# The first attention's softmax: query maxima by GpSimd's partition_all_reduce, row sums by more products with ones

## The chip, the core and the metric

The program runs on one core of a Trainium2 chip. The metric is the device time of one execution in microseconds (us). The time before is 1392.51 us, the median of 3 runs (1391.57 to 1392.85). Five engines work side by side, each with its own queue of instructions: TensorE (PE, with its weight loads as PEld), VectorE (DVE), ScalarE (ACT), GpSimd (POOL) and SyncE (SP, which issues DMAs). A name with a q, such as POOLq, is the engine's sequencer.

## The reference

The whole network is four layers of attention, mixing and feed-forward blocks over x of 4 x 128 x 128. The change touches only the first block, an attention with ternary weights over 2048 context rows for each of the 4 batches. `bitnet_linear` is a product of rounded inputs with ternary weights.

```python
vis = bitnet_linear(dinov2_features, W_d2v, b_d2v)
image_embeds = bitnet_linear(vis, W_img, b_img)
fused = bitnet_linear(text_embeddings, W_txt, b_txt)
for Wa, ba in ((W_att0, b_att0), (W_att1, b_att1)):
    kv = bitnet_linear(image_embeds, Wa, ba)
    k = jnp.concatenate([kv, kv], axis=-1)
    scores = jnp.einsum('bse,bpe->bsp', fused, k) * inv_sqrt_e
    attn = jax.nn.softmax(scores, axis=-1)
    fused = fused + 0.1 * jnp.einsum('bsp,bpe->bse', attn, k)
```

So for two rounds and four batches there is a softmax of 128 queries over 2048 keys, and its product with the keys themselves. The second round starts from the first round's result.

## The kernel before, in words

The block is `bit_attention` (from L935). It quantizes the context, makes the keys of both rounds (`k_ps` L1053 evicted by ACT at L1056, `v_ps` L1061 evicted by DVE at L1063), and then works through 8 units, one for each round and batch (L1148 on). A unit has its 2048 keys on the partitions, as 16 chunks of 128 keys; the 128 queries lie along the free dimension. Eight chunks make one PSUM tile `st` of 128 x 1024, so a unit has two halves, g = 0 and 1. For one unit:

- `queries` (L1078 to L1082): a product with `fold`, DVE scales it into `fq`; then DVE adds 0.1 times the key bias to `fused`.
- `scores` (L1092, L1094): 8 products into `st` for a half, and a DVE reduction over the 8 chunks into `mh`: for each partition and query the largest score.
- `top` (L1097 to L1101): DVE joins the two halves of `mh` (L1097); PE transposes it so that the queries lie on the partitions (`m_tr` L1099), and DVE takes the maximum for each query (`mq` L1101).
- `spread` (L1104, L1106): PE transposes `mq`, repeated 128 times, back (L1104), and ACT copies the result to SBUF as `mb`: the maximum of each query on every partition.
- `weights` (L1110 to L1120), for each half: DVE subtracts `mb` from `st` into `p` (L1110), ACT takes exp (L1112), and GpSimd adds up the eight chunks of `p` in three additions of 128 x 512, 128 x 256 and 128 x 128 (L1118, L1119, L1120) into `total`. For the last unit DVE does these additions.
- `values` (L1135 to L1145), one unit behind: 16 products `av` of `p` with the keys, two products of `total` with ones (`rsum` L1140), DVE's reciprocal and product (L1142, L1143), a product with `fold` (L1144), and DVE adds the result into `fused` (L1145).

The pipeline over the units is written out at the bottom: `top` of unit i, first half of the scores of unit i + 1, `spread` and `weights` of unit i, `values` of unit i - 1, second half of the scores of unit i + 1, `queries` of unit i + 2. After unit 2 comes `ternary(ps, 5, 7)`, which makes the ternary weights for the feed-forward (ACT sums at L960, product L965, DVE L966 to L974). After units 3 and 4 GpSimd turns a stretch of the mask into floats (`ctxT`, L1175). `st` has three PSUM buffers, the small tiles have two. After the units the largest magnitude of `fused` is found by DVE (L896, L900) and GpSimd (L903), and the feed-forward follows (L1198 on).

The order of the instructions on an engine is near the order of the source, but not the same: the framework that builds the program places an instruction earlier where its buffers allow. It also puts a pair of `MODIFY_POOL_CONFIG` records on GpSimd's queue wherever a `PARTITION_ALL_REDUCE` follows an addition or scaling by GpSimd, or the other way round. In the source nothing of this is seen; in the instruction order of a program it stands as one extra entry on GpSimd ahead of the first instruction of the new kind. Memsets and copies have none.

Of the kernel before, what the change touches and what calls it, by code (L numbers as in the profile page):

```python
# [9 lines left out]
F32 = mybir.dt.float32  # L10
BF16 = mybir.dt.bfloat16
# [3 lines left out]
ALU = mybir.AluOpType  # L15
AX = mybir.AxisListType.X
PSUM = bass.MemoryType.PSUM

P = 128
B = 4  # L20
T = 128
# [250 lines left out]
class Net:  # L272
# [662 lines left out]
    def bit_attention(self, nxt):  # L935


        nc, tc = self.nc, self.tc
        w = self.load("l0x")
        with ExitStack() as es:  # L940
            one = es.enter_context(tc.tile_pool(name="bit1", bufs=1))
            wk = es.enter_context(tc.tile_pool(name="bit2", bufs=2))
# [39 lines left out]
            ps = es.enter_context(tc.tile_pool(name="bit_ps", bufs=2, space=PSUM))  # L982
# [29 lines left out]
            total = one.tile([P, NS // W], F32, name="total")  # L1012
# [24 lines left out]
            HC = NCH // 2  # L1037
            rounds = []
            for r, n in enumerate(("att0", "att1")):
                kv = big.tile([P, BIG], F32, tag="big", name="kv")  # L1040
                kT = kv[:, 0 : NS // 2]
                v = kv[:, NS // 2 :].rearrange("p (c w) -> p c w", w=64)
                osc = out_scale(n, s_img)
                osc10 = self.small(1, "osc10" + n)
                nc.vector.tensor_scalar_mul(osc10, osc, 0.1)
                rounds.append((n, kT, v, osc10))
                pairs = qimg.rearrange("p (c h k) -> p c h k", h=2, k=P)
                for j in range(B):
                    mm = stp.tile([P, W], F32, tag="st", name="k_ps")
                    for lo in range(0, W, 512):  # L1050
                        at = (j * W + lo) // P
                        for h in range(2):
                            nc.tensor.matmul(  # L1053
                                mm[h * 64 : h * 64 + 64, lo : lo + 512], qw[:, L0X[n]], pairs[:, at : at + 4, h],
                                start=True, stop=True)
                    nc.scalar.activation(  # L1056
                        kT[:, j * W : j * W + W], mm, AF.Identity, bias=self.col("b_" + n), scale=osc)
                    mm = stp.tile([P, W], F32, tag="st", name="v_ps")
                    for i in range(NCH):
                        at = (j * NCH + i) * P  # L1060
                        nc.tensor.matmul(  # L1061
                            mm[:, i * 64 : i * 64 + 64], qimg[:, at : at + P], qw[:, L0X[n]], start=True, stop=True)
                    nc.vector.tensor_copy(  # L1063
                        v[:, j * NCH : j * NCH + NCH], mm.rearrange("p (c w) -> p c w", w=64))

            class Unit:
# [2 lines left out]

                def __init__(u, r, b):  # L1070
                    u.b = b
                    u.n, u.kT, u.v, u.osc10 = rounds[r]
                    u.fb = fused[:, b * T : b * T + T]
                    u.st, u.ts = [None, None], []

                def queries(u):
                    mm = ps.tile([P, 512], F32, tag="mm", name="fq_ps")
                    nc.tensor.matmul(mm[:, 0:T], self.flat(fold), u.fb, start=True, stop=True)  # L1078
                    u.q = wk.tile([P, T], F32, tag="fq", name="fq")
                    nc.vector.tensor_scalar_mul(u.q, mm[:, 0:T], 1.0 / math.sqrt(C))  # L1080
                    nc.vector.scalar_tensor_tensor(
                        u.fb, self.col("b_" + u.n).to_broadcast([P, T]), 0.1, u.fb, ALU.mult, ALU.add)  # L1082
                    u.mh = wk.tile([P, 2, P], F32, tag="mh", name="mh")
                    u.total = wk.tile([P, 2, P], F32, tag="total", name="total")

                def scores(u, g):
                    u.st[g] = stp.tile([P, 2, HC // 2, P], F32, tag="st", name="st")
# [7 lines left out]

                def top(u):
                    nc.vector.tensor_max(u.mh[:, 0], u.mh[:, 0], u.mh[:, 1])  # L1097
                    u.mm = ps.tile([P, 512], F32, tag="mm", name="m_tr")
                    nc.tensor.transpose(u.mm[:, 0:P], u.mh[:, 0], self.ident)  # L1099
                    u.mq = self.small(1, "mq")  # L1100
                    nc.vector.reduce_max(u.mq, u.mm[:, 0:P], axis=AX)  # L1101

                def spread(u):
                    nc.tensor.transpose(u.mm[:, P : 2 * P], u.mq.to_broadcast([P, P]), self.ident)  # L1104
                    u.mb = wk.tile([P, P], F32, tag="mb", name="mb")
                    nc.scalar.copy(u.mb, u.mm[:, P : 2 * P])  # L1106

                def weights(u, g):
                    p = tp.tile([P, HC, P], F32, tag="p", name="p")
                    nc.vector.tensor_sub(  # L1110
                        p, u.st[g].rearrange("p h c q -> p (h c) q"), bc_mid(u.mb, HC))
                    nc.scalar.activation(p, p, AF.Exp)  # L1112
                    u.ts.append(p)

                    half = p[:, 0 : HC // 2]
                    a = wk.tile([P, HC // 2, P], F32, tag="qtmp", name="psum")
                    eng = nc.vector if u is units[-1] else nc.gpsimd
                    eng.tensor_add(a, half, p[:, HC // 2 :])  # L1118
                    eng.tensor_add(a[:, 0:2], a[:, 0:2], a[:, 2:4])  # L1119
                    eng.tensor_add(u.total[:, g], a[:, 0], a[:, 1])  # L1120

                def values(u):
                    def bank(name):

                        if u is units[-1]:
                            return stp.tile([P, W], F32, tag="st", name=name)
                        return ps.tile([P, 512], F32, tag="mm", name=name)


                    av = bank("av")  # L1130
                    for g in range(2):
                        for c in range(HC // 2):
                            for h in range(2):
                                ch = u.b * NCH + 2 * (g * (HC // 2) + c) + h
                                nc.tensor.matmul(  # L1135
                                    av[h * 64 : h * 64 + 64, 0:T], u.v[:, ch], u.ts[g][:, h * (HC // 2) + c],
                                    start=g + c == 0, stop=g == 1 and c == HC // 2 - 1)
                    mm = bank("rsum")
                    for g in range(2):
                        nc.tensor.matmul(mm[:, 0:T], self.ones, u.total[:, g], start=g == 0, stop=g == 1)  # L1140
                    o = wk.tile([P, T], F32, tag="o", name="o")
                    nc.vector.reciprocal(o, mm[:, 0:T])  # L1142
                    nc.vector.tensor_mul(o, o, av[:, 0:T])  # L1143
                    nc.tensor.matmul(mm[:, T : 2 * T], self.flat(fold), o, start=True, stop=True)  # L1144
                    nc.vector.scalar_tensor_tensor(u.fb, mm[:, T : 2 * T], u.osc10, u.fb, ALU.mult, ALU.add)  # L1145

            units = [Unit(r, b) for r in range(2) for b in range(B)]
# [4 lines left out]
            for i, u in enumerate(units):  # L1152
                u.top()
                if i + 1 < len(units):
                    units[i + 1].scores(0)
                u.spread()
                u.weights(0)
                u.weights(1)
                if i:
                    units[i - 1].values()  # L1160
                if i + 1 < len(units):
                    units[i + 1].scores(1)
                if i + 2 < len(units):
                    units[i + 2].queries()
                if i == 2:
                    ternary(ps, 5, 7)
                if i in (3, 4):

                    half = NS // 2
                    lo = (i - 3) * half  # L1170
                    mw = wk.tile([P, 1024], I32, tag="qtmp", name="mask")
                    nc.sync.dma_start(
                        mw[DC:AUG], self.A["mask"][:, lo // 4 : (lo + half) // 4].partition_broadcast(3)[:, 0])
                    aug = self.k("augs")[DC:AUG]
                    nc.gpsimd.tensor_scalar(  # L1175
                        self.ctxT[DC:AUG, lo : lo + half], mw.bitcast(U8)[DC:AUG], aug[:, 0:1], aug[:, 1:2],
                        ALU.mult, ALU.add)
# [10 lines left out]
            self.quantize(wk, fused, qf, inv)  # L1188
            qa = one.tile([P, B], BF16, name="qa")
            self.quantize(wk, avg, qa, inv)  # L1190
            qab = one.tile([P, B, T], BF16, name="qab")
            nc.vector.tensor_copy(qab, bc_in(qa, T))
            hT = big.tile([P, BIG], F32, tag="big", name="hT")[:, 0 : 4 * N].rearrange("p (m n) -> p m n", m=4)
            osc = out_scale("f1", s)
# [1056 lines left out]
```

## Time and profile before

| What | Value |
|---|---|
| Median of 3 runs | 1392.51 us |
| Profiled execution's own time | 1393.84 us |
| Its span, first to last instruction | 1391.7 us |
| Mean granted TensorE clock over the span | 0.916 |
| The units' stretch, 85.9 to 151.4 us: DVE busy | 50.90 of 65.50 us |
| The same: PE busy | 48.82 us |
| The same: POOL busy | 41.39 us |
| The same: ACT busy | 19.86 us |
| The same: granted TensorE clock | 0.81 |

In a line of the timeline the columns are start, busy time, engine, line, operation, output and inputs, and in square brackets how long the engine had been idle and what ended that. In a table of groups, a count, the busy time and the mean ns of one stand ahead of the idle time. In a table of waits each row is the waiting engine and tile, what it waited for, the total in us, the number of times and the longest.

The eight copies of `mb` (L1106) start at 85.68, 93.64, 102.65, 114.82, 125.59, 135.08, 143.16 and 151.11 us. They mark the beat of the units.

### The profile page before, as it was taken

The page shows a single profiled execution, that of the slowest core. Times are in us where ns is not written, and L with a number is a line of the kernel's source. Part 1 is how long each engine was busy: PE and PEld are TensorE (multiplying, and loading weights), DVE is VectorE, ACT ScalarE, POOL GpSimd, SP SyncE. Part 2 cuts the span into 40 slices and gives each one's busy share as a digit, 9 for nine tenths or more (in the row PEclk, how much of TensorE's full clock was granted, in tenths as well). Part 3 has the DMA queues.
Part 4 walks back from the last instruction along what each step waited for, and adds up shares of the span by engine and source line. Part 5 has one row for each costly group of instructions (what it writes and reads, how often), then busy time and mean ns, then how long its engine had stood idle before and what let it go on. Part 6 is the DMA issues. An engine that isn't in the chain of part 4 may idle for free.

```text
span 1391.7 us, 15803 instructions
## 1 busy us (share of the span) xinstructions
PE 1149.7 (83%) x6204; PEld 604.2 (43%) x6204; DVE 914.2 (66%) x1596; ACT 627.0 (45%) x848; POOL 205.9 (15%) x187
## 2 busy tenths in 40 slices
PE   2477557677899999999998944899987889999978
PEld 0156422222644444444433424476342454666644
DVE  7988779899348666776676698512564776554535
ACT  3743256444346555665553410233542761545432
POOL 0026205357000001000000430000122200000000
PEclk9988768789999999999999976799998988999978
DMA  6000000000700000000000100330000000000010
GB/s 188 0 1 2 1 1 0 30 0 0 211 0 1 0 0 0 1 0 0 1 1 0 61 0 1 104 75 23 0 0 7 7 7 0 2 1 2 3 57 8
DMA packets 9485, 27.82 MB, mean 20 GB/s; under 512 B 1191, under 2 KB 7120, under 8 KB 8350
## 3 DMA queue, kind: packets, MB, share of 16 engines
q1 hardware_dynamic: 8286, 24.88, 6.2%
q10 hardware_dynamic: 1120, 1.88, 0.4%
q8 instruction: 51, 0.84, 0.3%
q14 instruction: 28, 0.23, 0.1%
HBM read 26.49 MB, written 0.26 MB: 19 GB/s over the span
## 4 chain that ended last, share of the span: by engine, by line
PE 61%; DVE 19%; ACT 5%; issue 5%; POOL 3%; DVEq 0%; ACTq 0%; POOLq 0%
PE sc L590 12%; PE av L614 12%; PE s_ps L780 5%; DVE h L1392 3%; PE t_ps L804 2%; PE k_ps L706 2%; PE h_ps L1831 2%; PE y_ps L1843 2%; PE av L817 2%; PE mm L1478 2%; PE y_ps L1397 1%; DVE dbu L1383 1%; PE q_ps L542 1%; POOL hc L1395 1%; POOL mbs L606 1%
## 5 line engine op out<-in xcount | busy, mean ns | idle before, releaser
L614 PE MATMUL av<-s,ctx 128*97 128x512 f32 x448 | 210.4, 601 | 11.6 <-ACT s L612 11.0
L590 PE MATMUL sc<-q_aug,ctxT 99*128 99x512 f32 x448 | 206.2, 592 | 0.0
L611 DVE TENSOR_TENSOR s<-s,mbs 128x1024 f32<-128x1024 f32 x112 | 133.0, 1220 | 39.0 <-POOL mbs L606 39.0
L592 ACT COPY s<-sc 128x1024 f32<-128x1024 f32 x112 | 112.3, 1003 | 80.7 <-PE sc L590 80.7
L612 ACT ACTIVATE s<-s 128x1024 f32<-128x1024 f32 x112 | 116.2, 1057 | 63.1 <-DVE s L611 62.8
L600 DVE TENSOR_TENSOR m<-m,s 128x1024 f32<-128x1024 f32 x72 | 88.2, 1225 | 75.0 <-ACT s L592 75.0
L590 PEld LDWEIGHTS sc<-q_aug,ctxT 99*128 99x128 f32 x448 | 84.6, 189 | 110.2 <-issue 91.3
L614 PEld LDWEIGHTS av<-s,ctx 128*97 128x97 f32 x448 | 72.5, 166 | 124.1 <-issue 103.6
L784 DVE TENSOR_REDUCE na_m<-s_ps 128x1 f32<-128x512 f32 x128 | 82.2, 686 | 61.9 <-PE s_ps L780 61.7
L606 POOL PARTITION_ALL_REDUCE mbs<-m x20 | 35.7, 1785 | 488.4 <-DVE m L602 488.4
L810 ACT ACTIVATE p<-t_ps 128x1024 f32<-128x1024 f32 x64 | 62.0, 1021 | 85.4 <-PE t_ps L804 85.4
L1397 PE MATMUL y_ps<-hc,consts 128*128 128x512 f32 x128 | 75.6, 724 | 29.2 <-POOL hc L1395 27.7
L1395 POOL TENSOR_TENSOR hc<-h,cs 128x1024 f32<-128x1024 f32 x32 | 75.7, 2378 | 84.1 <-DVE h L1392 84.1
L780 PE MATMUL s_ps<-kT,q 32*128 32x512 f32 x256 | 81.9, 682 | 1.0 <-DVE na_m L784 0.9
L1392 DVE TENSOR_TENSOR_SCAN h<-dA,dbu 128x512 f32<-128x512 f32 x64 | 74.2, 1205 | 4.1 <-ACT dA L1389 3.9
L1397 PEld LDWEIGHTS y_ps<-hc,consts 128*128 128x128 f32 x128 | 26.1, 223 | 82.0 <-POOL hc L1395 56.4
L804 PE MATMUL t_ps<-q,kT 32*128 32x128 f32 x1024 | 57.0, 287 | 1.2 <-ACT p L810 1.2
L1389 ACT ACTIVATE dA<-delta,A 128x508 f32<-128x508 f32 x64 | 42.8, 687 | 29.5 <-DVE h L1392 29.3
L804 PEld LDWEIGHTS t_ps<-q,kT 32*128 32x128 f32 x1024 | 48.6, 189 | 11.2 <-issue 7.0
L393 PEld LDWEIGHTS <-consts 128*128 128x128 bf16 x160 | 17.6, 120 | 67.4 <-issue 51.3
L1847 DVE SCALAR_TENSOR_TENSOR x<-y_ps,cw,x 128x128 f32<-128x128 f32 x32 | 9.0, 345 | 50.3 <-PE y_ps L1843 44.4
L780 PEld LDWEIGHTS s_ps<-kT,q 32*128 32x128 f32 x256 | 28.1, 194 | 25.4 <-DVE na_m L784 14.8
(599 smaller groups left out, 1949.5 us busy)
## 6 DMA issues: line engine op xcount, KB each, us to landing
w_moe<-in_moe SPq DMA_DIRECT2D x2, 2048.0 KB, 9.6
ctxT<-in_ctxT SPq DMA_DIRECT2D x3, 768.0 KB
w_l3f<-in_l3f SPq DMA_DIRECT2D x1, 1920.0 KB, 8.1
rows<-in_rows ACTq DMA_DIRECT2D x1, 1664.0 KB, 13.7
w_l0f<-in_l0f SPq DMA_DIRECT2D x1, 1024.0 KB
w_mamba<-in_mamba SPq DMA_DIRECT2D x1, 976.0 KB, 18.3
w_r<-in_r SPq DMA_DIRECT2D x1, 960.0 KB
consts<-in_consts SPq DMA_DIRECT2D x1, 832.0 KB, 16.6
```

The lines of the kernel that those rows point to most:

```text
L590: nc.tensor.matmul(sc[:, i], self.ctxT[:, at : at + P], u.q, start=True, stop=True)
L592: nc.scalar.copy(s, sc)
L600: nc.vector.tensor_max(u.m, u.m, u.s[j])
L611: nc.vector.tensor_sub(p, p, bc_mid(u.mb, 2))
L612: nc.scalar.activation(p, p, AF.Exp)
L614: nc.tensor.matmul(u.av[: DC + 1], self.ctx[:, u.b * NCH + chunks[2 * j + i]], p[:, i], start=j + i == 0, stop=j == n - 1 and i == 1)
L780: nc.tensor.matmul(t, qs[rows], kT[rows, s, j * 512 : j * 512 + 512], start=True, stop=True)
L784: nc.vector.tensor_reduce(part[:, at : at + 1], t, axis=AX, op=ALU.max, negate=True)
L804: nc.tensor.matmul(ts[g // 2][:, g % 2, j], kT[g * 32 : g * 32 + 32, s, at : at + P], qs[g * 32 : g * 32 + 32], start=True, stop=True)
L1392: nc.vector.tensor_tensor_scan(h[:, half], self.flat(dA), dbu[:, half], 0.0, ALU.mult, ALU.add)
L1395: nc.gpsimd.tensor_mul(hc, h, bc_mid(cs, 2))
L1397: nc.tensor.matmul(y[:, half], self.ident, hc[:, half], start=n == 0, stop=n == 15)
```

## The change

`top` now ends with one GpSimd `partition_all_reduce` of 128 x 128, which takes the maximum over the partitions and writes it to all of them as `mb`; the two transposes, `mq` and the copy by ACT are gone, and `spread` with them. Of the three additions by GpSimd for each half only the first is left; `total` is four times as large, and `values` sums its eight chunks with eight products with ones in place of two. For the last unit there are no additions at all, and 16 products with ones. Two smaller edits: the key bias times 0.1 is made once for a round (`b01`), so that the addition to `fused` is a `tensor_scalar`; and `qab` shares a buffer.

```diff
+                b01 = self.small(1, "b01" + n)
+                nc.vector.tensor_scalar_mul(b01, self.col("b_" + n), 0.1)
...
-                    nc.vector.scalar_tensor_tensor(
-                        u.fb, self.col("b_" + u.n).to_broadcast([P, T]), 0.1, u.fb, ALU.mult, ALU.add)
+                    nc.vector.tensor_scalar(u.fb, u.fb, u.b01, None, ALU.add)
...
-                    u.total = wk.tile([P, 2, P], F32, tag="total", name="total")
+                    u.total = wk.tile([P, 2, HC // 2, P], F32, tag="total", name="total")
...
                     nc.vector.tensor_max(u.mh[:, 0], u.mh[:, 0], u.mh[:, 1])
-                    u.mm = ps.tile([P, 512], F32, tag="mm", name="m_tr")
-                    nc.tensor.transpose(u.mm[:, 0:P], u.mh[:, 0], self.ident)
-                    u.mq = self.small(1, "mq")
-                    nc.vector.reduce_max(u.mq, u.mm[:, 0:P], axis=AX)
-
-                def spread(u):
-                    nc.tensor.transpose(u.mm[:, P : 2 * P], u.mq.to_broadcast([P, P]), self.ident)
                     u.mb = wk.tile([P, P], F32, tag="mb", name="mb")
-                    nc.scalar.copy(u.mb, u.mm[:, P : 2 * P])
+                    nc.gpsimd.partition_all_reduce(u.mb, u.mh[:, 0], P, bass_isa.ReduceOp.max)
...
-                    half = p[:, 0 : HC // 2]
-                    a = wk.tile([P, HC // 2, P], F32, tag="qtmp", name="psum")
-                    eng = nc.vector if u is units[-1] else nc.gpsimd
-                    eng.tensor_add(a, half, p[:, HC // 2 :])
-                    eng.tensor_add(a[:, 0:2], a[:, 0:2], a[:, 2:4])
-                    eng.tensor_add(u.total[:, g], a[:, 0], a[:, 1])
+                    if u is not units[-1]:
+                        nc.gpsimd.tensor_add(u.total[:, g], p[:, 0 : HC // 2], p[:, HC // 2 :])
...
-                    for g in range(2):
-                        nc.tensor.matmul(mm[:, 0:T], self.ones, u.total[:, g], start=g == 0, stop=g == 1)
+                    if u is units[-1]:
+                        parts = [u.ts[g][:, c] for g in range(2) for c in range(HC)]
+                    else:
+                        parts = [u.total[:, g, c] for g in range(2) for c in range(HC // 2)]
+                    for c, v in enumerate(parts):
+                        nc.tensor.matmul(mm[:, 0:T], self.ones, v, start=c == 0, stop=c == len(parts) - 1)
...
-                u.spread()
...
-            qab = one.tile([P, B, T], BF16, name="qab")
+            qab = one.tile([P, B, T], BF16, tag="xn", name="qab")
```

In the instruction order of the new program GpSimd has, for the units: the all-reduce of unit 0, a pair of `MODIFY_POOL_CONFIG`, two additions of 128 x 512, a pair, the all-reduce of unit 1, a pair, two additions, and so on to the all-reduce of unit 7. The two conversions of the mask stand after the all-reduces of units 3 and 4, behind the pair and ahead of the additions. ACT's two sums for `ternary` (L960) stand ahead of the last five and the last three evictions of keys (L1056), where they stood between the exps of units 2 and 3.

More of the change, by code (lines that the diff above doesn't have):

```diff
@@ L1045, in bit_attention @@
                 nc.vector.tensor_scalar_mul(osc10, osc, 0.1)
-                rounds.append((n, kT, v, osc10))
+                b01 = self.small(1, "b01" + n)
+                nc.vector.tensor_scalar_mul(b01, self.col("b_" + n), 0.1)
+                rounds.append((n, kT, v, osc10, b01))
                 pairs = qimg.rearrange("p (c h k) -> p c h k", h=2, k=P)
@@ L1071, in __init__ @@
                     u.b = b
-                    u.n, u.kT, u.v, u.osc10 = rounds[r]
+                    u.n, u.kT, u.v, u.osc10, u.b01 = rounds[r]
                     u.fb = fused[:, b * T : b * T + T]
```

## The prediction

> **What bounds the kernel now.** The page's first part says who is busy over the whole span, and seems to invite the change: GpSimd has 15%.
>
> ```profile
> PE 1149.7 (83%) x6204; PEld 604.2 (43%) x6204; DVE 914.2 (66%) x1596; ACT 627.0 (45%) x848; POOL 205.9 (15%) x187
> ```
>
> The change acts in one stretch, so I read the timeline there, first for the steady units 6 and 7.
>
> ```profile
> 143.16 0.27 ACT L1106 COPY mb<-m_tr 128x128 f32<-128x128 f32 x1 [3.74 <-PE m_tr L1104]
> 144.06 2.35 DVE L1110 TENSOR_TENSOR p<-st,mb 128x1024 f32<-128x1024 f32 x2
> ...
> 146.32 0.95 DVE L1142 RECIPROCAL o<-rsum 128x128 f32<-128x128 f32 x1
> 146.44 1.26 POOL L1118 TENSOR_TENSOR psum<-p 128x512 f32<-128x512 f32 x1 [2.83 <-ACT p L1112]
> 147.18 1.16 DVE L1094 TENSOR_REDUCE mh<-st 128x128 f32<-128x1024 f32 x1
> ...
> 151.11 0.27 ACT L1106 COPY mb<-m_tr 128x128 f32<-128x128 f32 x1 [3.62 <-PE m_tr L1104]
> 151.47 2.40 DVE L1110 TENSOR_TENSOR p<-st,mb 128x1024 f32<-128x1024 f32 x2 [1.81 <-ACT mb L1106]
> ```
>
> DVE goes from one step to the next: a unit takes 8 us and DVE is busy for 7.4 of it (two reductions 2.4, two subtractions 2.4, reciprocal 0.95, and six steps of about 0.3). GpSimd waits for exps. The waits of the same stretch show what the two transposes cost:
>
> ```profile
> POOL psum L1118 <- ACT p L1112: 47.5, 7, 28.3
> ACT mb L1106 <- PE m_tr L1104: 35.4, 8, 5.7
> ...
> DVE p L1110 <- ACT mb L1106: 3.6, 3, 1.8
> ```
>
> ACT's 35.4 us are idle time of an engine with little to do. What the next in line, DVE, waits for `mb` is 3.6 us in all. So the removed steps are worth some us and no more.
>
> Then GpSimd's own timeline, at the place where it changes from additions to an all-reduce, and the groups of its all-reduces:
>
> ```profile
> 151.15 0.45 POOL L1120 TENSOR_TENSOR total<-psum 128x128 f32<-128x128 f32 x1
> 159.65 0.38 POOL L903 PARTITION_ALL_REDUCE am_f_g<-am_f_m  x1 [8.04 <-DVE am_f_m L900]
> 160.80 0.35 POOL L903 PARTITION_ALL_REDUCE am_f_g<-am_f_m  x1 [0.77 <-DVE tf_f L671]
> ```
> ```profile
> L606 POOL PARTITION_ALL_REDUCE mbs<-m x20 | 35.7, 1785 | 488.4 <-DVE m L602 488.4
> ```
> ```profile
> L903 POOLq MODIFY_POOL_CONFIG  x4: 11/11/11, 1.5 to 151.8; - x4
> L1118 POOLq MODIFY_POOL_CONFIG  x2: 83/83/83, 60.1 to 60.1; - x2
> ```
>
> The last two rows are those of lines 903 and 1118. At 60.1 us and at 151.8 us, right behind the last instruction of the old kind (ends 60.11 and 151.60), GpSimd's queue runs a pair of `MODIFY_POOL_CONFIG`. The records take 11 or 83 ns, but I read them as the start of a load of other code. Each pair of before lies in a long idle stretch of GpSimd, so the trace can't say what it takes, only what it can't exceed.
>
> **The change, part by part.** The new instruction order has 14 such pairs in the units, two between each all-reduce and the next, where before had 2 up to the end of the units. Let G be the time from the end of one kind to the start of the other where no data is late.
>
> *All-reduce of 128 x 128.* Not in the trace. It lies between 0.35 us for 128 x 1 (L903) and 1.785 us for 128 x 512 (L606); on a straight line 0.35 + 127/511 x 1.435 = 0.71 us. The Trainium skill speaks against it: GPSIMD Engine Reference, section 3.2, gives 247.7 us for a `tensor_reduce` of [128, 2048] along the partitions, 0.121 us an element, so some 15.5 us for 128; by that the eight would add 118 us. But L606 is this very instruction with 512 elements in 1.785 us; I take 0.71.
>
> *Additions on GpSimd.* Two of 1.27 us (L1118) stay for a unit, 2.55 us; the L1119 and L1120 steps (0.72 and 0.45, twice) go, 2.35 us of GpSimd's time, which nothing waited for but ACT's L960 (2.9 us, through their buffer).
>
> *G.* Below, nothing but the records: 0.02 us. Above, the gap of 8.04 us at 151.6, which the row puts down to DVE: L900 ended at 159.51, the all-reduce started 0.14 us later, so the load was over by then. Into the additions' kind the narrowest gap is wider, 12.38 us ahead of L1944. The GPSIMD Engine Reference, section 2.1, says that the first call to freshly loaded code pays about 6 us, measured 5.95 us from `MODIFY_POOL_CONFIG` to the first instruction, with no visible record. No run here shows it; by that price alone the sum below is 1442 us. I take the middle of 5.95 and 8.04, 7.0 us: the page's price lacks the issue of the pair (0.2 us at 151.6) and is for unnamed code.
>
> *The beat.* GpSimd's queue is in order, so all-reduce i + 1 stands behind additions i, and these behind exp i and all-reduce i. Everything is a single ring: all-reduce 0.71, G, additions 2.55, G. That is 3.26 + 2G, 17.3 us for a unit where the beat was 8. The data isn't late: the first exp ends 2.4 us after the all-reduce (1.22 + 1.06 and the hand-over), inside the first G; the next `mh` some 5.2 us after it (two subtractions, one reduction, one maximum), inside the rest. Behind the waiting all-reduce are queued the additions and the two mask conversions; for it wait DVE's subtraction, ACT's exp and PE's `av`.
>
> *Sum for the units.* The first all-reduce can start at 83.9 us (the old L1097 of unit 0 ended at 83.78) and needs no pair, as its code is resident from L903. Seven beats of 3.26 + 2G, twice a mask conversion of 3.76 us (L1175, now inside the ring), and the last all-reduce: the last `mb` is there at 83.9 + 22.8 + 14G + 7.5 + 0.7 = 114.9 + 14G, with G = 7 at 212.9 us. Before it was there at 151.38. So +61.5 us.
>
> *More products with ones.* Six more for each of seven units, 0.12 us each (L1135 runs 32 records, 16 products, in 1.97 us): 0.7 us of PE in a ring that leaves PE idle; nothing. If GpSimd weren't the bound it would still lie under DVE's 7.4 us.
>
> *After the last `mb`.* Before: 8.65 us until `fused` starts at 160.03. Now DVE has no additions, but 16 products with ones follow the last `av`, on a PE that had idled: at 160 to 163 us, after an idle us or two, the granted clock was 0.50, and 26 `av` records took 2.73 us in place of some 1.6. Between +0.5 (full clock) and +4 us; I take +2.
>
> *Ahead of the units.* ACT's two sums L960 (1.06 + 0.19 + 0.63 + 0.19 = 2.07 us) move in among the evictions of keys, where ACT is busy 75% and DVE 88%. Between 0 and 2.07; I take 1. The chain they led (L965 to L974) is now under a wait for `mb`. `b01` and `qab`: some tenths of us on DVE at most, under other work.
>
> *In all* 61.5 + 2 + 1 = +64.5 us. On the profiled execution's 1393.84 us that is 1458.3; the median of the runs stands 1.3 us below that execution, so 1457. The later stages only move.
>
> **The rivals.** In general the time is 1359 + 14G, as long as 3.26 + 2G is over 7.4.
>
> *The switch hides, as it does now: faster.* If G is 2.07 us or less, DVE sets the beat. The unit loses `mq` (0.28) and the waits for the transposes: 7.2 us of work and 0.2 of gaps, 7.4 us for a beat. Seven beats make 51.8, `ternary` 3.7 us of DVE, together 55.5 where the eight copies of `mb` span 65.4: about -9, 1384 us. For it: no switch of before has cost anything that can be seen, and the pair starts as soon as the queue comes to it. Against: the page's 5.95 us, and that now no idle stretch is left around it. The time crosses the old one at G = 2.4 us.
>
> *A shorter load.* G between 2.4 and 5.5 us: slower, by less; at 4 us 1415.
>
> *A longer load.* The code of the additions may be larger, and only 12.38 us bound it: with 10 us for it and 8 for the other, 7 x 18 in place of 14G, 1485 us.
>
> **How the numbers follow.** G of 5.5 to 8.1 us: chance 0.78, 1436 to 1473 us. A shorter load 0.07, a longer 0.09, the hidden switch 0.06. The range takes G from 5.4 to 8.3 us, 1434 to 1476 us, and leaves out some 2 in 10. Faster by over 0.2% (about what a measurement of this kernel can tell from no change) 0.05, within it 0.01, slower 0.94.
>
> **What would show it.** In the changed profile, 14 pairs of `MODIFY_POOL_CONFIG` more or less evenly over the stretch; GpSimd's all-reduces 17 us apart, 21 for units 4 and 5; idle gaps on GpSimd of about 7 us, put down to nothing or to an engine long done; DVE's `p` waiting for POOL's `mb`, some 60 us and more; all-reduces of 0.7 us each. The prediction is wrong if the all-reduces come 8 us apart, if one of 128 x 128 takes several us, or if the two directions differ much.

## The result and the profile after

The changed kernel takes 1451.58 us, the median of 6 runs (1449.1 to 1456.03), where the kernel before takes 1392.68 us in the runs beside them. The ratio is 1.0423, with a 95% interval of 1.041 to 1.0435: slower by 58.9 us. The profiled execution took 1450.15 us (before: 1393.84).

GpSimd's own timeline of the changed kernel has the whole story. L1100 is the all-reduce, L1110 an addition of 128 x 512, L1168 a mask conversion (lines behind L1145 stand 7 lower than before).

```profile
84.53 0.73 POOL L1100 PARTITION_ALL_REDUCE mb<-mh  x1 [23.66 <-DVE mh L1098]
92.68 2.48 POOL L1110 TENSOR_TENSOR total<-p 128x512 f32<-128x512 f32 x2 [7.43 <-issue]
100.98 0.72 POOL L1100 PARTITION_ALL_REDUCE mb<-mh  x1 [5.82 <-issue]
109.24 2.47 POOL L1110 TENSOR_TENSOR total<-p 128x512 f32<-128x512 f32 x2 [7.53 <-PE av L1125]
117.59 1.66 POOL L1100 PARTITION_ALL_REDUCE mb<-mh  x1 [5.88 <-issue]
...
141.95 3.76 POOL L1168 TENSOR_SCALAR ctxT<-mask,consts 3x4096 f32<-3x4096 uint8 x1 [6.81 <-PE av L1125]
145.80 2.49 POOL L1110 TENSOR_TENSOR total<-p 128x512 f32<-128x512 f32 x2
154.45 0.72 POOL L1100 PARTITION_ALL_REDUCE mb<-mh  x1 [6.17 <-issue]
...
206.53 0.72 POOL L1100 PARTITION_ALL_REDUCE mb<-mh  x1 [6.04 <-issue]
```

Read the numbers in brackets. Ahead of every all-reduce but the first GpSimd was idle for 5.8 to 6.2 us, ahead of every first addition or conversion for 6.7 to 7.5, and the releaser is "issue" (nothing that the profile shows) or something long done. Of the 122.7 us from the first all-reduce's start to the last one's end (84.53 to 207.25), 91.0 are these 14 gaps. The rest is the work: 17.4 us of additions, 7.5 of conversions, 6.7 of all-reduces, and some 0.2 us between them. The groups of the three lines count the pairs, seven in each direction:

```profile
L1100 POOLq MODIFY_POOL_CONFIG  x14: 1/1/11, 95.4 to 200.7; - x14
L1110 POOLq MODIFY_POOL_CONFIG  x10: 98/98/98, 85.2 to 191.1; - x10
L1168 POOLq MODIFY_POOL_CONFIG  x4: 98/98/98, 135.1 to 155.2; - x4
```

The records last 1 to 98 ns, and the first ones stand right where the old kind ends (85.2 where the all-reduce ends at 85.26, 95.4 behind the additions that end at 95.16). What follows them, some 6 or 7 us, has no record of its own. That it is a load of code is a reading that no view shows: the profiles of both kernels count the same 9485 DMA packets, 51 of them on the queue for instructions. What is seen is a gap that comes with each pair. I call it the switch.

The waits of the stretch show that it is easy to miss:

```profile
...
DVE o L1136 <- PE rsum L1134: 50.8, 8, 9.5
POOL mb L1100 <- issue: 35.7, 6, 6.2
...
PE rsum L1134 <- POOL total L1110: 15.1, 6, 5.1
DVE p L1104 <- POOL mb L1100: 14.9, 7, 3.1
POOL total L1110 <- PE av L1125: 14.4, 2, 7.5
POOL total L1110 <- issue: 14.3, 2, 7.4
```

DVE's largest row puts its idleness down to PE's row sums. But these waited for `total`, which is GpSimd's. The end of the units shows the order:

```profile
198.01 2.48 POOL L1110 TENSOR_TENSOR total<-p 128x512 f32<-128x512 f32 x2 [6.91 <-issue]
199.31 2.38 PE L1134 MATMUL rsum<-total,ones 128*128 128x128 f32 x16 [1.21 <-POOL total L1110]
201.74 0.96 DVE L1136 RECIPROCAL o<-rsum 128x128 f32<-128x128 f32 x1 [5.65 <-PE rsum L1134]
...
207.28 2.36 DVE L1104 TENSOR_TENSOR p<-st,mb 128x1024 f32<-128x1024 f32 x2 [2.09 <-POOL mb L1100]
```

DVE takes its instructions in this order, and the reciprocal stands ahead of the next subtraction. So most of the time in which DVE would wait for `mb` was spent at the reciprocal. DVE's row that names GpSimd has 14.9 us only.

What follows the last `mb`, in the timeline of all engines:

```profile
208.60 2.21 ACT L1106 ACTIVATE p<-p 128x1024 f32<-128x1024 f32 x2 [13.94 <-DVE p L1104]
209.71 3.68 PE L1125 MATMUL av<-p,kv 128*64 128x128 f32 x32 [6.04 <-ACT p L1106]
213.32 4.68 PE L1134 MATMUL rsum<-p,ones 128*128 128x128 f32 x32
...
219.90 0.35 DVE L1139 SCALAR_TENSOR_TENSOR fused<-rsum,osc10att,fused 128x128 f32<-128x128 f32 x1 [0.58 <-PE rsum L1138]
```

From the last `mb` to the end of this `fused` are 13.0 us; before it were 9.0 (151.38 to 160.38). PE comes out of 6 us of idleness: the granted clock is 0.50 while `av` runs (209.7 to 213.3 us), and the 16 products with ones come behind it.

### The profile page after: what moved, and what is told of

It reads as the page before. It is cut to its first block, busy times and chain, and to the rows that moved or that the text cites. A ratio compares the mean times of both kernels' runs of the same rounds, so it can differ in the third digit from the quotient of the medians.

```text
span 1448.1 us, 15963 instructions
## 1 busy us (share of the span) xinstructions
PE 1163.3 (80%) x6289; PEld 623.8 (43%) x6300; DVE 910.2 (63%) x1584; ACT 624.7 (43%) x840; POOL 195.1 (13%) x167
## 2 busy tenths in 40 slices
DMA packets 9485, 27.82 MB, mean 19 GB/s; under 512 B 1191, under 2 KB 7120, under 8 KB 8350
## 4 chain that ended last, share of the span: by engine, by line
PE 60%; DVE 21%; issue 6%; ACT 6%; POOL 5%; DMA 1%; DVEq 0%; ACTq 0%; POOLq 0%
PE av L614 12%; PE sc L590 12%; PE s_ps L780 5%; DVE h L1385 3%; PE t_ps L804 2%; PE h_ps L1824 2%; PE y_ps L1836 2%; PE av L817 2%; PE k_ps L706 2%; PE y_ps L1390 2%; PE st L1093 1%; POOL hc L1388 1%; PE mm L1471 1%; PE q_ps L542 1%; DVE dbu L1376 1%
## 5 line engine op out<-in xcount | busy, mean ns | idle before, releaser
L1106 ACT ACTIVATE p<-p 128x1024 f32<-128x1024 f32 x16 | 16.9, 1057 | 112.0 <-DVE p L1104 111.4
L1093 PE MATMUL st<-fq,kv 64*128 64x128 f32 x256 | 27.3, 395 | 29.9 <-DVE p L1104 29.8
L393 PEld LDWEIGHTS <-consts 128*128 128x128 bf16 x160 | 17.4, 119 | 67.0 <-issue 50.5
## 6 DMA issues: line engine op xcount, KB each, us to landing
consts<-in_consts SPq DMA_DIRECT2D x1, 832.0 KB, 17.4
```

## The experiments

The table has all runs. "Block end" is the start of DVE's L915 behind the units in the profiled execution, against 161.38 us before. Pairs are those between the first all-reduce or addition of the units and the last. Ratios are to the kernel before, beside which each was run.

| Run | Pairs | Block end | Median, us | Ratio (95%) |
|---|---|---|---|---|
| changed kernel | 14 | +59.9 | 1451.58 | 1.0423 (1.041 to 1.0435) |
| switch_only | 13 | +58.4 | 1448.98 | 1.0389 (1.0374 to 1.0404) |
| tail_on_dve | 14 | +57.4 | 1448.62 | 1.039 (1.0375 to 1.0404) |
| half_switches | 8 | +25.3 | 1417.65 | 1.0161 (1.014 to 1.0182) |
| first_unit_only | 1 | +1.0 | 1397.35 | 1.0024 (1.0012 to 1.0036) |
| maxima_alone | 0 | +6.2 | 1399.96 | 1.0057 (1.0038 to 1.0076) |
| maxima_dve_adds | 0 | +7.4 | 1396.45 | 1.0026 (1.0015 to 1.0038) |
| sums_alone | 0 | +15.8 | 1409.19 | 1.012 (1.0094 to 1.0146) |
| small_edits | 0 | +0.7 | 1393.63 | 1.0009 (0.9999 to 1.0019) |
| no_pair_16 | 0 | 0.0 | 1397.36 | 1.0028 (1.0018 to 1.0038) |
| no_pair_12 | 0 | -0.9 | 1391.28 | 0.9979 (0.9967 to 0.9991) |
| no_pair_8 | 0 | +0.2 | 1392.22 | 0.9986 (0.9976 to 0.9996) |
| no_pair_12_late | 0 | +1.3 | 1397.38 | 1.0029 (1.0018 to 1.004) |

A difference of 3 us or less in the median is not the block's alone: runs of one kernel lie up to 14 us apart, and the block end of the profiled execution doesn't follow the median there (no_pair_16 has 0.0 and +3.6). So I read small differences at the block end, large ones in both. Even the block end carries some chance: the all-reduce ahead of the units (L903), which comes before every edit, starts at 59.62 to 61.86 us in the runs (before: 59.76), so a difference of 2 us or less there is not by itself the block's.

**The pairs alone.** The theory: each pair costs GpSimd 6 to 7 us wherever the queue meets it, and the ring of GpSimd's work sets the beat. A rival: the all-reduce is costly because it now lies between DVE's maximum and DVE's subtraction.

```diff
                     eng.tensor_add(u.total[:, g], a[:, 0], a[:, 1])
+                    if g == 1 and u is not units[-1]:
+                        nc.gpsimd.partition_all_reduce(
+                            self.small(1, "idle_g"), u.total[:, 1, 0:1], P, bass_isa.ReduceOp.max)
```

> The kernel before with its transposes, additions and row sums, and nothing added but one GpSimd all-reduce of 128 x 1 behind each of the first seven units' additions. Its result is used by nothing. It brings 14 pairs of MODIFY_POOL_CONFIG, as in the changed kernel, and takes 0.35 us a time itself. If a pair costs GpSimd 6 to 7 us wherever it stands (theory), a unit takes GpSimd 4.9 us of additions, 0.35 and 13 us of switching, 18.2 us in place of a beat of 8, and the row sums of every unit wait for it: time 1449 us, between 1435 and 1462, slower than before by 3 to 5%. If the cost lay in the all-reduce being on the path of the maxima, or in the hand-overs between DVE and GpSimd, and not in the pair (rival), it stays under 1400 us.

Measured: 1448.98 us. Seven all-reduces of 0.38 us each, used by nothing, do what the whole change did, as the theory had it (1449). They bring 13 pairs between them and the additions; a fourteenth, ahead of the first additions, lies in an idle stretch as before. The timeline of GpSimd in this kernel:

```profile
144.96 2.49 POOL L1118 TENSOR_TENSOR psum<-p 128x512 f32<-128x512 f32 x2 [6.92 <-issue]
147.42 1.41 POOL L1119 TENSOR_TENSOR psum<-psum 128x256 f32<-128x256 f32 x2
148.79 0.86 POOL L1120 TENSOR_TENSOR total<-psum 128x128 f32<-128x128 f32 x2
155.63 0.38 POOL L1122 PARTITION_ALL_REDUCE idle_g<-total  x1 [5.98 <-issue]
163.17 3.76 POOL L1178 TENSOR_SCALAR ctxT<-mask,consts 3x4096 f32<-3x4096 uint8 x1 [7.16 <-issue]
```

The seven lie between 101.85 and 218.40 us; less the two conversions of 3.8 us, six beats take 18.2 us each, as the sum said. An all-reduce of 128 x 1 has the same gap ahead of it (mean 5.86 us) as one of 128 x 128 (5.94), so it doesn't come with the size of the data. The rival, which had under 1400 us, is out.

**Half of the pairs.** GpSimd adds for units 0, 2, 4 and 6 only; the others take 16 products with ones, and the mask conversions stand ahead of the units.

```diff
-                    if u is not units[-1]:
+                    if units.index(u) % 2 == 0:
                         nc.gpsimd.tensor_add(u.total[:, g], p[:, 0 : HC // 2], p[:, HC // 2 :])
```

> Additions on GpSimd for units 0, 2, 4 and 6 only, 16 products with ones for the others, mask conversions ahead of the units: 8 pairs between the units' all-reduces in place of 14. Theory: two units take 0.72 + 7.1 + 2.5 + 5.9 and one free beat of 7.4, 23.6 us; four such, against eight free beats of 7.4, cost 35 us over maxima_alone: 1418 to 1432. Rival (all-reduce on the path, or contention on GpSimd's port): no step of 8 us between the two kinds of units.

Measured: 1417.65 us, just under the theory's 1418 to 1432. One kernel shows both beats:

```profile
104.75 0.72 POOL L1100 PARTITION_ALL_REDUCE mb<-mh  x1 [5.80 <-issue]
110.64 0.70 POOL L1100 PARTITION_ALL_REDUCE mb<-mh  x1 [5.16 <-DVE mh L1098]
119.12 2.48 POOL L1110 TENSOR_TENSOR total<-p 128x512 f32<-128x512 f32 x2 [7.78 <-issue]
127.38 0.72 POOL L1100 PARTITION_ALL_REDUCE mb<-mh  x1 [5.78 <-DVE o L1136]
134.97 0.70 POOL L1100 PARTITION_ALL_REDUCE mb<-mh  x1 [6.86 <-DVE mh L1098]
```

16.7 us from one all-reduce to the next with two pairs between (110.64 to 127.38), 5.9 and 7.6 us without. There the gap is a wait for `mh`, the data. The rival, which had no step between the two kinds of units, is out. The 8 pairs cost the block 19 us more than none (maxima_alone), the 14 cost 54: two units with two pairs between them take some 23 us (104.75 to 127.38) in place of 2 x 9.4, as the free unit makes up for a part. I had expected 35 us over maxima_alone. The pair of units is near what I had (22.6 us, expected 23.6), but the beat without pairs, in maxima_alone, is 9.4 us and not 7.4.

**The maxima alone, without pairs.** GpSimd does no additions; 16 products with ones for every unit, the mask conversions ahead of the units. The second kernel does the first addition of each half by DVE, with 8 products.

```diff
-                    if u is not units[-1]:
-                        nc.gpsimd.tensor_add(u.total[:, g], p[:, 0 : HC // 2], p[:, HC // 2 :])
```
```diff
-                        nc.gpsimd.tensor_add(u.total[:, g], p[:, 0 : HC // 2], p[:, HC // 2 :])
+                        nc.vector.tensor_add(u.total[:, g], p[:, 0 : HC // 2], p[:, HC // 2 :])
```

> The all-reduces stay, GpSimd has no additions: all units sum their weights by 16 products with ones, and the two mask conversions stand ahead of the first all-reduce, so no pair of MODIFY_POOL_CONFIG lies between the units' all-reduces. Theory (the code switch is the whole loss): beat of 7.4 to 8.2 us, set by DVE or by PE with its 10 more products, all-reduces of 0.72 us, time 1380 to 1395. Rival (the all-reduce and its hand-over on the path to the subtraction cost): still at least 20 us slower than before, with DVE waiting for mb by 2 us or more in each unit.

> As maxima_alone, but the first additions (128 x 512, 0.69 us each) on DVE and eight products with ones. Theory: DVE sets the beat, 7.4 + 1.4 = 8.8 us, less the transposes' waits; seven beats of 8.8 and 3.7 us of ternary work give 65.3 where before had 65.4: 1388 to 1400. Rival (all-reduce on the path): 1410 or more.

Measured: 1399.96 and 1396.45 us. The rival, 20 us slower or more, is out in both. The first kernel is above the theory's 1395 too, the second lies in its range. Over 50 us of the loss are gone with the pairs, but no gain is there. Two reasons are mine. The conversions end at 82.32 us, their pair follows, and the first all-reduce starts 5.81 us later, though `mh` was there at 86.76:

```profile
74.80 7.52 POOL L1145 TENSOR_SCALAR ctxT<-mask,consts 3x4096 f32<-3x4096 uint8 x2 [13.11 <-DMA mask<-in_mask]
...
86.49 0.27 DVE L1097 TENSOR_TENSOR mh<-mh 128x128 f32<-128x128 f32 x1
...
88.13 0.72 POOL L1099 PARTITION_ALL_REDUCE mb<-mh  x1 [5.81 <-DVE mh L1094]
```

And the last unit's 16 products stand behind the last `mb`: from there to the end of `fused` are 11.9 us, where before had 9.0. The beat in between averages 9.4 us with 16 products and 9.6 with 8, not the 7.4 to 8.2 and 8.8 of the theory, and no shorter than before (9.35).

**The sums alone.** The transposes stay, the sums are the changed kernel's; GpSimd has additions only, and so no pair.

```diff
-                    nc.gpsimd.partition_all_reduce(u.mb, u.mh[:, 0], P, bass_isa.ReduceOp.max)
+                    nc.scalar.copy(u.mb, u.mm[:, P : 2 * P])
```

> The transposes stay, only the sums are changed (one addition on GpSimd for a half, eight products with ones, 16 for the last unit). No new pair. Theory: within 6 us of before, 1387 to 1398: 0.7 us more PE for a unit under DVE, the last unit's 16 products some 1 to 3 us later, ACT's sums no longer behind the additions' buffer. Rival (the products on a half-clocked PE cost): slower by 8 us or more.

Measured: 1409.19 us, 16.8 us slower. My theory (within 6 us of before) missed; the rival held. Of the 15.8 us at the block end 10.5 lie between the first and the last `mb` (75.9 us, before 65.4), and 4.4 behind the last, where the 16 products of the last unit stand. PE's timeline for one unit:

```profile
139.64 0.47 PE L1104 MATMUL m_tr<-consts,mq 128*128 128x128 f32 x1
140.04 2.54 PE L1131 MATMUL av<-p,kv 128*64 128x128 f32 x32
142.51 2.05 PE L1140 MATMUL rsum<-total,ones 128*128 128x128 f32 x16
```

Eight products with ones (16 records) take 2.05 us, 0.256 us each. I had priced them at 0.12, from `av`, whose products use 64 columns and lie two side by side. So a unit has 1.5 us more of PE, not 0.7. The windows of the last units (in order: time, PE, PEld, DVE, ACT and POOL busy with counts, granted clock, DMA) of before, of this kernel and of maxima_alone show what comes with it:

```profile
125.60:151.10 25.50, 19.44 (x212) 16.00 (x214) 20.73 (x31) 7.13 (x9) 20.95 (x19) 0.90 0.01 2
```
```profile
128.30:162.50 34.20, 29.41 (x248) 24.44 (x250) 21.09 (x31) 7.14 (x9) 7.50 (x6) 0.80 0.00 1
```
```profile
125.50:154.00 28.50, 27.65 (x306) 24.43 (x304) 20.67 (x28) 6.34 (x6) 2.08 (x3) 1.00 0.01 2
```

Three units each. DVE has the same work in all three. With 8 products PE is busy for 86% at a clock of 0.80, and a unit takes 11.4 us; with 16 it is busy for 97% at full clock, and a unit takes 9.5. More work for PE, and a shorter beat. Before, DVE was the longer one (20.73 of 25.50). The kernels differ in their transposes too, so that the clock's part of the 2 us isn't shown apart. Between the two kernels without transposes the clock falls as well, from 0.95 with 16 products to 0.82 with 8 (90 to 150 us), but their beats are nearly the same, and DVE has more to do in the second. The Trainium skill has a rule for the clock (TensorE: Matmul & The Clock Gate, section "What's actually happening"): half rate after an idle window of about 3.4 us, full rate under sustained work. The trace agrees in part. In the kernel with the sums alone the granted clock fell from 1.00 to 0.50 near 137.7 us, and the longest idle gap of PE in the 11 us before was 1.1 us.

**The tail.** The changed kernel, with the last unit's additions by DVE as before.

```diff
+                    else:
+                        a = u.total[:, g]
+                        nc.vector.tensor_add(a, p[:, 0 : HC // 2], p[:, HC // 2 :])
+                        nc.vector.tensor_add(a[:, 0:2], a[:, 0:2], a[:, 2:4])
+                        nc.vector.tensor_add(a[:, 0], a[:, 0], a[:, 1])
```

> The changed kernel, with the additions of the last unit made by DVE in three steps and its row sums by two products with ones, as in the kernel before. If the 4.0 us by which the end of the last unit got longer are the 16 products with ones on a slowed-down PE (theory), the stretch from the end of the last maxima to the update of fused falls from 13.0 to 9 to 10 us and the time from 1451.6 to 1447.5 to 1449 us. If the stretch is long because av is slow after the idle ring (rival), it stays at 12 us or more and the time within 1 us of 1451.6.

Measured: 1448.62 us, and 8.8 us from the last `mb` to the end of `fused` (208.99 to 217.75), a little less than the theory's 9 to 10. The theory held, and the rival (12 us or more, for a slow `av`) is out:

```profile
211.46 3.40 PE L1130 MATMUL av<-p,kv 128*64 128x128 f32 x32 [5.81 <-ACT p L1106]
214.79 0.71 PE L1139 MATMUL rsum<-total,ones 128*128 128x128 f32 x4
```

`av` is as slow as in the changed kernel (3.40 against 3.68 us), and the 4.68 us of products are 0.71. The stretch is then no longer than before, though `av` is slower than there. Before, the values of the unit ahead stood in the same stretch:

```profile
154.49 0.95 DVE L1142 RECIPROCAL o<-rsum 128x128 f32<-128x128 f32 x1
...
160.03 0.35 DVE L1145 SCALAR_TENSOR_TENSOR fused<-rsum,osc10att,fused 128x128 f32<-128x128 f32 x1 [0.27 <-PE rsum L1144]
```

The reciprocal at 154.49 is unit 6's. In the slow ring that work is done before the last `mb` comes.

**One pair, and the small edits.** The kernel before with unit 0 alone by the all-reduce; and the kernel before with `b01` and `qab` alone.

```diff
                 def top(u):
                     nc.vector.tensor_max(u.mh[:, 0], u.mh[:, 0], u.mh[:, 1])
+                    if u is units[0]:
+                        u.mb = wk.tile([P, P], F32, tag="mb", name="mb")
+                        nc.gpsimd.partition_all_reduce(u.mb, u.mh[:, 0], P, bass_isa.ReduceOp.max)
+                        return
```
```diff
-                    nc.vector.scalar_tensor_tensor(
-                        u.fb, self.col("b_" + u.n).to_broadcast([P, T]), 0.1, u.fb, ALU.mult, ALU.add)
+                    nc.vector.tensor_scalar(u.fb, u.fb, u.b01, None, ALU.add)
```

> The kernel before, with the maxima of unit 0 alone taken by GpSimd's all-reduce, whose code is still there from the quantization; all other units by transposes. The number of pairs stays as before: the one that stood ahead of the units now stands behind the first all-reduce. If a pair costs about 7 us from where the queue reaches it, hidden where GpSimd has slack (theory), the additions of unit 0 start at about 92 us in place of 87.5, GpSimd makes up for it within two or three units, and the gain is the two transposes of one unit: 1390 to 1393.5 us. If the delay of the first sums goes through to the end (rival), +3 to +6 us: 1395.5 to 1398.5.

> The kernel before with only the two small edits: 0.1 times the key bias made once a round, and qab in a shared buffer. Maxima and sums as before. Theory: nothing that can be measured, 1391 to 1394 us. Rival: the new order of ACT's sums for the ternary weights and of the eviction of keys comes with these edits and delays the first unit, +1.5 to +3 us.

Measured: 1397.35 and 1393.63 us. With one pair, GpSimd's timeline has

```profile
84.75 0.73 POOL L1100 PARTITION_ALL_REDUCE mb<-mh  x1 [24.21 <-DVE mh L1097]
92.52 2.49 POOL L1124 TENSOR_TENSOR psum<-p 128x512 f32<-128x512 f32 x2 [7.04 <-issue]
```

and the additions are back at waiting for exps by 106.45 us. At the block end +1.0 us is left of those 7. The median, +4.5 us, says more than that; by its number the rival's range is met, but the profiled execution took 1392.56 us and its block end doesn't show it. Where the rest lies was not found. The small edits make no difference at the resolution of the runs (0.9999 to 1.0019), as the theory had it.

**No pair at all, and a fair start.** Now the two faults of the maxima's kernels are mended: ACT converts the mask, and the last unit's additions are DVE's as before. 16, 12 and 8 products with ones for each other unit; the rest of the sums is done by DVE.

```diff
-                    nc.gpsimd.tensor_scalar(
-                        self.ctxT[DC:AUG, lo : lo + half], mw.bitcast(U8)[DC:AUG], aug[:, 0:1], aug[:, 1:2],
-                        ALU.mult, ALU.add)
+                    nc.scalar.activation(
+                        self.ctxT[DC:AUG, lo : lo + half], mw.bitcast(U8)[DC:AUG], AF.Identity,
+                        bias=aug[:, 1:2], scale=aug[:, 0:1])
```
```diff
+                        if g in (0,):
+                            nc.vector.tensor_add(u.total[:, g], p[:, 0 : HC // 2], p[:, HC // 2 :])
```

> GpSimd does nothing in the units but the all-reduces, so that there is no pair at all: the mask conversions by ACT in one activation each, the sums of units 0 to 6 by 16 products with ones, those of the last unit by DVE's three steps and two products. In the earlier run with 16 products the first maxima came 3.6 us late, behind the mask conversions and their pair, the beat was 9.4 us, PE the bound. With the first maxima at 84.5 us and the same beat the last come at 150.4 and the tail is as before: 1391 to 1393 us, between 1389 and 1395. If ACT's conversions or a slower PE take it back (rival), 1396 us or more.

> As no_pair_16, but DVE adds the two halves of the first eight chunks in one addition of 128 x 512 (0.69 us), so 12 products with ones. PE had 9.2 us of work in a unit at full clock with 16 products, of 0.256 us each: 8.2 us with 12. DVE had 6.9 us, now 7.6. If the longer of the two sets the beat (theory) it is 8.3 to 8.6 us, some 5 us less in all than with 16: 1385 to 1389 us, faster than before. If PE falls back to a lower granted clock once it has gaps, as it did with 8 products on the row of sums alone (rival), the beat is 9.3 us or more and the time 1392 to 1396.

> As no_pair_16, but DVE adds both halves (two of 0.69 us), 8 products with ones. PE 7.2 us at full clock, DVE 8.3 us. The earlier run with the same sums had beats of 9.6 us at a granted clock of 0.82. Theory (the longer of the two): beat 8.5 to 9, 1387 to 1391. Rival (the lower clock of a PE with gaps sets the beat): 9.6 us, 1393 to 1397.

Measured: 1397.36, 1391.28 and 1392.22 us. The first maxima come at 84 to 85 us, as meant. With 16 products the block ends where it did before, to the hundredth of a us, though the median is 3.6 us above: the time falls in the rival's range, yet the loss isn't in the block, where the rival had it. With 12, GpSimd's timeline is

```profile
109.27 0.70 POOL L1100 PARTITION_ALL_REDUCE mb<-mh  x1 [8.36 <-DVE wscale L967]
119.51 0.70 POOL L1100 PARTITION_ALL_REDUCE mb<-mh  x1 [9.54 <-DVE mh L1098]
132.06 0.70 POOL L1100 PARTITION_ALL_REDUCE mb<-mh  x1 [11.84 <-DVE mh L1098]
141.05 0.70 POOL L1100 PARTITION_ALL_REDUCE mb<-mh  x1 [8.29 <-DVE mh L1098]
149.78 0.70 POOL L1100 PARTITION_ALL_REDUCE mb<-mh  x1 [8.02 <-DVE mh L1098]
```

Steady beats of 9.0 and 8.7 us, not the 8.3 to 8.6 of the theory, and 12.55 ahead of 132.06. It is faster than before by 0.21% (0.09 to 0.33), less than I expected; with 8 products it is 0.14% (0.04 to 0.24). But the units aren't shorter: from the first to the last `mb` the three take 65.3, 65.8 and 66.1 us, before 65.4. Where the 2.5 us of the medians lie was not found. Both times lie between those of theory and rival; from 90 to 150 us PE's granted clock was 0.93 and 0.91, and 0.99 with 16 products. As ACT's conversion lay between the two exps of the unit with the long beat, I moved it.

```diff
-                if i in (3, 4):
...
             self.quantize(wk, self.flat(hT), self.flat(qh), inv)
+            half = NS // 2
...
+                self.ctxT[DC:AUG, lo : lo + half], mw.bitcast(U8)[DC:AUG], AF.Identity,
+                bias=aug[:, 1:2], scale=aug[:, 0:1])
```

> As no_pair_12, but ACT converts the mask in the feed-forward, where it waits, and not between two exps of units 3 and 4. With no_pair_12 one conversion of 3.79 us lay between the two exps of unit 3, and the beat there was 12.55 us where the steady ones were 8.7 to 9.0. Theory: that beat falls to 9 to 9.5 us, some 3 us; of the two conversions one lies in a gap of 2.6 us of ACT, one in a gap of 3.6 us, so that 1 to 1.5 us come back: 1388 to 1390.5 us, faster than before by 0.2 to 0.4%. If DVE's work for the ternary weights, in the same stretch, sets that beat anyway (rival), the gain is gone and the time is 1391 to 1393.

Measured: 1397.38 us; my theory fell, and the time is above the rival's range too. The beat in question is 13.5 us (120.74 to 134.25) without the conversion, so that wasn't its cause. What is, stays open. And the two conversions, 7.5 us of ACT, hold up the next stage, where DVE now waits 4.40 us for ACT. The block's +1.3 us is less than the 2.1 us by which its L903 already started later.

## Why the prediction was right, and where not

**What sets the beat: right.** GpSimd's ring with two switches in a unit was the bound, and the data was never late. All-reduces came 16.0 to 16.8 us apart (predicted 17.3), 20.0 for units 4 and 5 (predicted 21). That the pairs do it, and not the place of the all-reduce, switch_only shows. What happens in the gap, a load of code or something else, no run tells apart.

**The size of G: 6.5 us, not 7.0.** It is two sizes. Into the all-reduce 5.94 us (5.82 to 6.17), into the additions or conversions 7.06 (6.72 to 7.53). The Trainium skill's 5.95 us (GPSIMD Engine Reference, section 2.1) fits the first and is 1.1 us short for the second; the 8.04 us that served as ceiling was partly the wait for data that its row named. That the two directions differ much was to be a sign against the prediction. They differ by 1.1 us, and one G for both was too simple. 14G was to be 98 us and was 91.0: this is more than the 5.4 us by which the forecast was high. Every return to a kind that had run 16 to 20 us earlier paid in full, where the page speaks of the first call.

**The instructions: right.** All-reduce 0.72 us against 0.71 on the straight line; the estimate of 15.5 us, from the rate in section 3.2 of the same page, was over 20 times too high. One of the eight, unit 2's, took 1.66 us, and 1.60 in tail_on_dve. In both kernels DVE ran L974 beside it (117.38 to 118.66 us in the changed kernel), and beside no other; that the two hinder each other was not tried. Additions 2.48 us for two against 2.55, conversions 3.76.

**The products with ones: wrong, at no cost here.** A product takes 0.256 us, twice what I took, for the reason found with the sums alone. In the slow ring PE idled and hid it. The step "if GpSimd weren't the bound it would still lie under DVE's 7.4 us" is wrong: in sums_alone, with the transposes, the units take 10.5 us longer. The rival of the hidden switch looks too large as well: with no pair in the way, the best of four versions gains 2.5 us, not 9. They don't test it as it stands, as they pay for the sums on DVE or PE.

**The tail: +4.0 us, not +2,** the upper end of its range. Of the two reasons that I gave, the 16 products make all of it: tail_on_dve gave back 4.2 us at this place (4.0 of them the products, 4.68 against 0.71), and 3.0 in the medians. `av` at half clock is there as foreseen, 3.68 us against 1.97, but tail_on_dve has it too and ends its stretch 0.2 us sooner than before. The row that I took for it was misread in its place: the 26 `av` records in 2.73 us stand at 151.0 us, at a clock of 0.50 as well, and from 160 to 163 us PE has no work.

**The start: +0.6 us, not +1** (84.53 against 83.9). The L903 ahead of the units was 0.76 us later already (60.52 against 59.76), so that ACT's two sums cost nothing that shows.

**The sum.** At the end of the block 55.9 us to the last `mb` and 4.0 behind it, +59.9 us; predicted 62.5 and 2, +64.5. The terms: -7.0 for the switches, +1.0 for the slow all-reduce, -0.3 for additions and conversions, -0.4 for the start, +2.0 for the tail; together -4.7, where the difference is -4.6 by the rounded terms. The median is +58.9. That it came so close is in part luck: the switches were 7.0 us too high, and the tail and the slow all-reduce gave 3.0 of them back.

**What would show it.** 14 pairs, gaps of about 7 us and all-reduces of 0.7 us are there. The wait of DVE's `p` for `mb`, 60 us and more, is not: 14.9, with 50.8 under another name, for the reason given with the waits.

## What to carry to other kernels

Count the changes of kind on GpSimd's queue before its instructions: here a pair with 0.2 us of records at most and 6 to 7 us behind it cost nothing that shows in an idle stretch, and set the beat where two of them stood in every turn of a loop. A price taken from a neighbour's row (here the products with ones, from `av`) has to be for the same shape, and a step that hides under one bound must be priced again for the next bound. And when a wait names an engine, ask what that engine itself waited for: here the stall was booked on the first instruction in DVE's queue that met it (50.8 us), not on the one that needed GpSimd's result (14.9).

## What the runs showed of the hardware

- The switch has a direction: into the all-reduce 5.94, 5.86 and 5.86 us on average (changed kernel, switch_only, half_switches), into additions and conversions 7.06, 7.15 and 7.34. Why, was not tried. The length of the pair's records doesn't tell the directions apart: in the units 1 to 11 ns against 82 to 98, but 11 ns ahead of the additions of L1395 in the kernel before.
- The switch doesn't wait for the data of the instruction behind it. In maxima_alone the all-reduce started 1.4 us after its `mh`, and 5.8 us after the conversions; in the changed kernel the exps of unit 0 ended at 88.92 us, in the middle of the first gap (85.26 to 92.68), and the additions started 3.8 us later.
- Fewer products with ones left PE with gaps, and its granted clock was lower: 0.82 with 8 against 0.95 with 16 (maxima_dve_adds, maxima_alone), 0.91 against 0.99 (no_pair_8, no_pair_16), all from 90 to 150 us. The beat was no shorter for them: 9.6 against 9.4 us, 9.4 against 9.3. As DVE had more work with 8, the clock's part in that isn't shown.
